# A graph network layer: the low-numbered sources of two aggregation steps by products with count matrices in place of row gathers

## The chip, the cores and the metric

The kernel runs on one core of a Trainium2 chip. The metric is the device time of one execution in microseconds (us), the median of three executions. A profile of one execution gives the busy times of the engines: PE (TensorE, products), DVE (VectorE), ACT (ScalarE), POOL (GpSimd) and the DMA queues that POOL, ACT and SP (SyncE) feed.

## What is computed

There are N = 10000 nodes with 512 float32 features, and E = 160000 directed edges, sorted by destination; a node has 16 incoming edges in the mean. The program is a relational graph layer with a feed-forward part, and after it two SAGE steps (the "last two steps"). The reference, cut to those two steps:

```python
def _sage_layer(h, src, dst, W_self, W_neigh, b, n_nodes):
    agg = segment_sum(h[src], dst, num_segments=n_nodes)       # sum the source rows of each node
    deg = segment_sum(ones_like(dst), dst, num_segments=n_nodes)
    h_neigh = agg / maximum(deg, 1.0)[:, None]
    return relu(h @ W_self + h_neigh @ W_neigh + b)

h = _sage_layer(feats, src, dst, W_self1, W_neigh1, b1, n_nodes)   # step 0
h = _sage_layer(h, src, dst, W_self2, W_neigh2, b2, n_nodes)       # step 1
```

Ahead of them, the first layer computes five products per node (`self_W` and four `rel_W`), and sums for every edge the row of its source and its edge type, `h_all[src, edge_type]`, by destination; then layer norms and a 512-1024-512 feed-forward part with a GELU follow.

## The kernel before

The nodes are cut into 78 blocks of 128 and one of 16. The kernel has four stages in time: the node products (in which the lists of edges are built as well, beside the products), the aggregation of the first layer with the feed-forward part, step 0, and step 1.

A block sums its edges in two ways. The first 11 edges of each of its 128 nodes are read by 11 indirect DMAs ("own" gathers: lane p of the gather is node p of the block), and DVE adds the 11 tiles to the sum. What a node has beyond 11 goes to 5 further gathers whose lanes are in any order, and to two "tails" that 4 and 16 blocks share; those tiles are added by products with one-hot matrices, on PE. Every gather moves 128 rows of 2 KB.

```python
T = 11 * E // (16 * N)          # 11 own edges a node
OT = 5                          # 5 gathers of other edges a block; 3 in the last, short block
SPANS = (4, 16)                 # a tail for 4 blocks, and one for 16

def gather(b, table):
    def rows(n, idx, name="rows", bufs=RING):                  # RING = 28 row tiles
        t = gat.tile([P, D], F32, name=name, bufs=bufs)
        nc.gpsimd.indirect_dma_start(out=t[:n], in_=table, ...)            # L660
        return t[:n]
    ...                                                        # tails, others, then own
def sums(b, others, hot):
    for t in order:                                            # 5 others and 2 tails
        nc.tensor.matmul(pa[:r], hot[:, t, :r], others[t], ...)            # L687
def add(b, pa, mine):
    for t in mine:                                             # 11 own tiles
        nc.vector.tensor_tensor(pa[:r], pa[:r], t[:r], op=OP.add)          # L699
```

The loop of the last two steps (`h_d` is the step's input, `wss` and `wns` its weights; `transposed` makes four transposes on PE, L167, and a copy on ACT, L168):

```python
for i, b in enumerate(blocks):
    hot = hots(blocks[i + 1])                                  # L676, DVE
    pa, mine = held
    add(b, pa, mine)                                           # L699, DVE
    nc.scalar.activation(m[:r], pa[:r], AF.Copy, scale=rdeg)   # L1021, ACT
    for k in range(KC):                                        # KC = 4
        nc.tensor.matmul(po[:r], hT[:, k, :r], wss[:, k, :])   # L1025
    if before:
        finish(*before)        # 4 products with wns (L991), bias, relu, store of block i-1
    turn(blocks[i + 1])        # transposes of the next block's own rows hb
    held = begin(blocks[i + 1], hot, h_d)                      # gathers and L687 of the next
    transposed(psT, mT[:, :, :r], m[:r], r)
    before = (b, po, mT)
```

The node products, beside which the lists are built a part at a time (`next(step)`), from windows of the sorted edges; each product is evicted by DVE:

```python
nc.vector.tensor_tensor(h, h, bself[:r], op=OP.add)                        # L614
nc.vector.tensor_tensor(xg[:r, c, :], xg[:r, c, :], ln2b[:r], op=OP.add)   # L615
for j, w in enumerate([wself] + wrel):                         # 5 weights
    for k in range(KC):
        nc.tensor.matmul(pm[:r], hT[:, k, :r], w[:, k, :], ...)            # L620
    ... nc.vector.tensor_tensor(...)                           # L623 and L626, the eviction
...
if b0 + c >= 2:
    next(step, None)           # a part of the lists, once a block
```

Of the kernel before, what the change touches and what calls it, by code (L numbers as in the profile page):

```python
# [8 lines left out]
F32 = mybir.dt.float32  # L9
# [12 lines left out]
def kernel(  # L22
# [32 lines left out]

    nc = tc.nc
# [18 lines left out]


    T = 11 * E // (16 * N)
    OT = 5
    OT_LAST = 3
# [3 lines left out]

    ROUNDS = 12
    PAD = P

    W = 36
    TAGS = 4 + 3 * NL
    FAR = 2 * SPAN * P
    WT = 2 * W + TAGS  # L90
    assert N % P and R * N <= 1 << 16 and 2 * T + WT <= 2 * P and OT * WT <= 512
    assert (4 + 3 * NL) * NB <= 1024 and 3 * NL * NB <= 512
    assert 4 * OT * P <= R * N and OT_LAST < OT and full % 2 == 0

    def own(b):

        return T if b < full else 0

# [13 lines left out]

    ident = const.tile([P, P], F32, name="ident")
# [9 lines left out]


    row = const.tile([P, full, T], I32, name="row")
    orow = const.tile([P, NB, OT], I32, name="orow")
    srow = [const.tile([P, -(-full // n)], I32, name=f"srow{i}") for i, n in enumerate(SPANS)]
    loc = const.tile([P, NB, OT + NL], F32, name="loc")
    fits = const.tile([1, 1], I32, name="fits")
    bad = const.tile([P, 5], F32, name="bad")  # L130
# [39 lines left out]
    def runs(ep, ep2, pse, found):  # L170
# [137 lines left out]
        nc.vector.tensor_tensor(deg, first[:, 1:], first[:, :P], op=OP.subtract)  # L308

# [25 lines left out]
        bounds = ep.tile([NB, 3 * NL, P], F32, name="bounds")  # L335
        nc.vector.tensor_copy(first_over, over)
        done = 0
        for lv, n in enumerate(SPANS):
# [22 lines left out]
            for i, v in enumerate((ov, upto)):  # L361
                w = bounds[:, 3 * lv + i, :]
                nc.vector.tensor_scalar(w, bounds[:, 3 * lv - 3 + i, :] if lv else v,
                                        float(-P if lv else -OT * P), 0.0, op0=OP.add, op1=OP.max)
                nc.vector.tensor_scalar(w, w, skip, None, op0=OP.add)
            nc.vector.tensor_scalar(bounds[:, 3 * lv + 2, :], ov, shift, 64.0, op0=OP.add,
                                    op1=OP.add)
            nc.vector.tensor_scalar(bounds[:, 3 * lv + 2, :], bounds[:, 3 * lv + 2, :], 0.0, None,
                                    op0=OP.max)
            yield  # L370
        for names, vs in ((("first", "deg", "from", "upto"), (first[:, :P], deg, ov, upto)),
                          ([f"{k}{lv}" for lv in range(NL) for k in ("sfrom", "supto", "sbase")],
                           [bounds[:, i, :] for i in range(3 * NL)])):
            pt = pse.tile([P, 512], F32, name="pe")
            for i, v in enumerate(vs):
                nc.tensor.transpose(pt[:, i * NB:(i + 1) * NB], v, ident[:NB, :NB])
            for i, name in enumerate(names):
                nc.vector.tensor_copy(found[name], pt[:, i * NB:(i + 1) * NB])

        nc.vector.memset(bad[:, 3:5], 0.0)  # L380
# [3 lines left out]
        nc.vector.tensor_scalar(bad[:NB, 3:4], upto_b, float(-P), over, op0=OP.is_lt, op1=OP.add)  # L384
        nc.vector.tensor_reduce(room, deg, op=OP.max, axis=mybir.AxisListType.X)
        nc.vector.tensor_tensor(room, room, lanes_b, op=OP.subtract)
        nc.vector.tensor_scalar(bad[:NB, 4:5], room, float(W), None, op0=OP.is_gt)
        pf = pse.tile([P, 512], F32, name="pe")
        nc.tensor.matmul(pf[:1, :5], ones[:, :1], bad, start=True, stop=True)
        count = ep.tile([1, 1], F32, name="count")  # L390
        nc.vector.tensor_reduce(count, pf[:1, :5], op=OP.add, axis=mybir.AxisListType.X)
        nc.vector.tensor_scalar(fits, count, 0.0, None, op0=OP.is_equal)
# [4 lines left out]
    def lists(ep, ep2, pse, found):  # L397

        tags = ep.tile([P, NB, TAGS], F32, name="tags")
        tag_i = ep.tile([P, NB, TAGS - 2], I32, name="tag_i")  # L400
        nc.vector.memset(tags[:, :, 0:1], 1.0)
        nc.gpsimd.iota(tags[:, :, 1], pattern=[[0, NB]], base=0, channel_multiplier=1,
                       allow_small_or_imprecise_dtypes=True)
        for i, n in enumerate(SPANS):
            of = tag_i[:, :, 2 + 2 * NL + i]
            nc.gpsimd.iota(of, pattern=[[1, NB]], base=0, channel_multiplier=0)
            nc.vector.tensor_scalar(of, of, n - 1, None, op0=OP.bitwise_and)
        for i, name in enumerate(["from"] + [f"sbase{lv}" for lv in range(NL)]):
            hi, lo = tag_i[:, :, 2 * i], tag_i[:, :, 2 * i + 1]
            nc.vector.tensor_copy(lo, found[name])  # L410
            nc.vector.tensor_scalar(hi, lo, 4, None, op0=OP.logical_shift_right)
            nc.vector.tensor_scalar(lo, lo, 15, None, op0=OP.bitwise_and)
        nc.vector.tensor_copy(tags[:, :, 2:], tag_i)
        nc.vector.memset(orow[:, full:, :], 0)
        nc.vector.tensor_scalar(rdeg, found["deg"], 1.0, None, op0=OP.max)
        nc.vector.reciprocal(rdeg, rdeg)
        iota_s = ep.tile([P, OT * P], F32, name="iota_s")
        nc.gpsimd.iota(iota_s, pattern=[[1, OT * P]], base=0, channel_multiplier=0,
                       allow_small_or_imprecise_dtypes=True)
        of_span = ep.tile([P, SPAN], F32, name="of_span")  # L420
        nc.gpsimd.iota(of_span, pattern=[[P, SPAN]], base=0, channel_multiplier=0,
                       allow_small_or_imprecise_dtypes=True)
        slot = ep.tile([P, OT], F32, name="slot")
        nc.gpsimd.iota(slot, pattern=[[P, OT]], base=0, channel_multiplier=1,
                       allow_small_or_imprecise_dtypes=True)
        nowhere = ep.tile([P, T], I32, name="nowhere")
        nc.gpsimd.iota(nowhere, pattern=[[0, T]], base=N * R, channel_multiplier=R)
        zero = ep.tile([P, D], F32, name="zero")
        nc.gpsimd.memset(zero, 0.0)
        for r in range(R):  # L430
            nc.sync.dma_start(hall_d[N:, r * D:(r + 1) * D], zero)
        nc.sync.dma_start(h1_d[N:, :], zero)
        nc.sync.dma_start(h2_d[N:, :], zero)

        kept, beyond = [], [None] * NL

        def between(low, high, b, n, out):

            after = ep2.tile([P, OT * P], BF16, name="after")
            if isinstance(out, str):  # L440
                out = ep2.tile([P, OT * P], BF16, name=out)[:, :n]
            nc.vector.tensor_scalar(after[:, :n], iota_s[:, :n], low[:, b:b + 1], None,
                                    op0=OP.is_ge)
            nc.vector.scalar_tensor_tensor(out, iota_s[:, :n], high[:, b:b + 1], after[:, :n],
# [3 lines left out]
        def picked(pm, at, base, place):  # L448


            n = at.shape[1]
# [26 lines left out]

        def read(b0):


            n = min(2, NB - b0)
            at = ep.tile([P, 2], I32, name="at", bufs=5)
# [13 lines left out]

        def look_up(b0, nb, win):
            halves = win.rearrange("p b j -> p (b j)").bitcast(BF16).rearrange(
                "p (b j) -> p b j", b=2)[:, :nb]  # L500
            ours, t0 = slice(b0, b0 + nb), own(b0)

            nc.vector.tensor_copy(halves[:, :, 2 * (t0 + W):2 * (t0 + W) + TAGS], tags[:, ours])

            if t0:
                few = ep2.tile([P, 2, T], I32, name="few")
                nc.vector.scalar_tensor_tensor(row[:, ours], halves[:, :, 0:2 * T:2], 256.0,
                                               halves[:, :, 1:2 * T:2], op0=OP.mult, op1=OP.add)
                nc.vector.tensor_tensor(few, found["deg"][:, ours].unsqueeze(2).to_broadcast(
                    [P, nb, T]), lane[:, None, :T].to_broadcast([P, nb, T]), op=OP.is_le)  # L510
                nc.vector.copy_predicated(row[:, ours], few,
                                          nowhere[:, None, :].to_broadcast([P, nb, T]))
            for c in range(nb):
                nt = OT if b0 + c < full else OT_LAST
                of = between(found["from"], found["upto"], b0 + c, nt * P, "of")
                pm = pse.tile([P, OT, WT], F32, name="pe")
                for t in range(nt):
                    nc.tensor.matmul(pm[:, t, :], of[:, t * P:(t + 1) * P],
                                     halves[:, c, 2 * t0:2 * t0 + WT], start=True, stop=True)
                got, rows, none = picked(pm[:, :nt], slot[:, :nt], 0, 2)  # L520
                nc.vector.tensor_tensor(loc[:, b0 + c, :nt], got[:, :, 1], none, op=OP.add)
                nc.vector.tensor_copy(orow[:, b0 + c, :nt], rows)
            if not t0:
                return

            for c in range(nb):
# [817 lines left out]
```

## Time and profile before

The three executions took 7276.59, 7280.13 and 7287.77 us; the median is 7280.13. The profiled execution has a span of 7287.9 us and a mean granted PE clock of 0.878 of full speed. The four stages, cut where the trace shows the first instructions of the next one:

| stage | from, to (us) | length | PE busy | DVE busy | POOL busy |
|---|---|---|---|---|---|
| node products, lists | 0 to 1590 | 1590 | 1483.7 | 915.6 | 84.3 |
| first aggregation, feed-forward | 1590 to 3575 | 1985 | 1704.3 | 1224.7 | 1250.8 |
| step 0 | 3575 to 5431 | 1856 | 1233.6 | 735.8 | 1228.8 |
| step 1 | 5431 to 7288 | 1857 | 1208.9 | 782.1 | 1242.6 |

How to read it: busy time is time in which an engine executed. For PE it is made of pipelined products whose ends are modelled, so the distance from the start of one product to the start of the next says more than the mean of one. For POOL, busy time holds the part of an indirect DMA that the engine itself works on, without the short gap that follows each of them; the moving of the rows is in the DMA columns.

### The profile page before, as it was taken

The page shows a single profiled execution, that of the slowest core. Times are in us where ns is not written, and L with a number is a line of the kernel's source. Part 1 is how long each engine was busy: PE and PEld are TensorE (multiplying, and loading weights), DVE is VectorE, ACT ScalarE, POOL GpSimd, SP SyncE. Part 2 cuts the span into 40 slices and gives each one's busy share as a digit, 9 for nine tenths or more (in the row PEclk, how much of TensorE's full clock was granted, in tenths as well). Part 3 has the DMA queues.
Part 4 walks back from the last instruction along what each step waited for, and adds up shares of the span by engine and source line. Part 5 has one row for each costly group of instructions (what it writes and reads, how often), then busy time and mean ns, then how long its engine had stood idle before and what let it go on. Part 6 is the DMA issues. An engine that isn't in the chain of part 4 may idle for free.

```text
span 7287.9 us, 49954 instructions
## 1 busy us (share of the span) xinstructions
PE 5630.5 (77%) x14251; PEld 2543.5 (35%) x14251; DVE 3658.1 (50%) x7302; ACT 1016.8 (14%) x1667; POOL 3806.5 (52%) x3927
## 2 busy tenths in 40 slices
PE   8999999976899888897676666666666666666666
PEld 3444444433334333343333233333232233332232
DVE  5457777334666666665344344333333444444444
ACT  1000000002233223232211011001010000000000
POOL 0000010026666666666266666666656666666665
PEclk9999999987999999998888888888887888887888
DMA  4222222246677777776366666666666777777775
GB/s 156 101 99 99 104 94 93 93 142 191 214 222 225 227 218 225 225 228 207 125 199 207 207 207 208 207 207 204 207 205 206 218 220 218 218 217 216 221 220 171
DMA packets 456993, 1361.47 MB, mean 187 GB/s; under 512 B 71746, under 2 KB 71746, under 8 KB 446578
## 3 DMA queue, kind: packets, MB, share of 16 engines
q0 software_dynamic: 308768, 1008.91, 46.8%
q1 hardware_dynamic: 136146, 266.29, 10.3%
q10 hardware_dynamic: 11792, 82.97, 2.8%
q8 instruction: 114, 1.87, 0.1%
q14 instruction: 173, 1.42, 0.1%
HBM read 1150.89 MB, written 207.01 MB: 186 GB/s over the span
## 4 chain that ended last, share of the span: by engine, by line
PE 34%; issue 21%; another core or an unknown queue 19%; ACT 3%; DVE 3%; POOL 2%; DMA 2%; ACTq 0%; POOLq 0%; DVEq 0%; SPq 0%
PE pa L687 9%; PE ph L783 6%; PE pm L620 5%; PE po L794 5%; PE po L991 3%; PE po L1025 3%; DVE pa L699 2%; POOL rows L660 2%; PE pT L167 1%; ACT hTb L168 1%; DMA rows<-h_d,row 1%; ACT mTb L168 1%; ACT mb L1021 0%; PE pT L771 0%
## 5 line engine op out<-in xcount | busy, mean ns | idle before, releaser
L699 DVE TENSOR_TENSOR pa<-pa,rows 128x512 f32<-128x512 f32 x2574 | 1798.6, 699 | 906.1 <-issue 571.5
L660 POOL DMA_INDIRECT rows<-h_d,row x1716 | 1669.4, 973 | 906.0 <-issue 423.0
L1025 PE MATMUL po<-wss,hTb 128*128 128x512 f32 (+1 forms) x1264 | 710.5, 715 | 652.1 <-ACT hTb L168 536.3
L687 PE MATMUL pa<-rows,hot 128*128 128x512 f32 (+1 forms) x2358 | 1096.2, 611 | 55.5 <-issue 31.9
L660 POOL DMA_INDIRECT rows<-hall_d,row x858 | 855.9, 998 | 492.6 <-issue 196.3
L620 PE MATMUL pm<-wrel,hT 128*128 128x512 f32 (+1 forms) x2528 | 1101.0, 593 | 14.4 <-DVE ha L623 14.4
L991 PE MATMUL po<-wns,mTb 128*128 128x512 f32 (+1 forms) x1264 | 662.0, 673 | 439.0 <-ACT mTb L168 306.3
L660 POOL DMA_INDIRECT rows<-h_d,orow x786 | 754.6, 960 | 400.8 <-issue 218.9
L620 PEld LDWEIGHTS pm<-wrel,hT 128*128 128x128 f32 (+1 forms) x2528 | 478.0, 189 | 622.1 <-issue 595.9
L687 PEld LDWEIGHTS pa<-rows,hot 128*128 128x128 f32 (+1 forms) x2358 | 458.9, 195 | 665.2 <-issue 631.6
L783 PE MATMUL ph<-x1T,w1s 128*128 128x512 f32 (+2 forms) x1344 | 587.0, 590 | 117.9 <-ACT hid L785 88.4
L1025 PEld LDWEIGHTS po<-wss,hTb 128*128 128x128 f32 (+1 forms) x1264 | 277.8, 231 | 1024.0 <-ACT hTb L168 589.5
L660 POOL DMA_INDIRECT rows<-hall_d,orow x393 | 373.3, 950 | 450.3 <-SPq L1340 326.5
L794 PE MATMUL po<-w2s,hid 128*128 128x512 f32 (+1 forms) x1264 | 560.9, 595 | 30.5 <-issue 23.2
L991 PEld LDWEIGHTS po<-wns,mTb 128*128 128x128 f32 (+1 forms) x1264 | 266.8, 216 | 816.2 <-issue 483.0
L687 PE MATMUL pa<-tail,hot 128*128 128x512 f32 x936 | 469.0, 617 | 78.0 <-issue 72.7
L997 DVE TENSOR_TENSOR po<-po,bss 128x512 f32<-128x512 f32 (+1 forms) x79 | 55.0, 696 | 805.5 <-remote 705.9
L493 POOL DMA_INDIRECT win<-rec_d,at x79 | 74.9, 948 | 719.7 <-issue 631.4
L623 DVE TENSOR_TENSOR ha<-pm,brel 128x512 f32<-128x512 f32 (+1 forms) x316 | 217.1, 687 | 424.1 <-PE pm L620 424.0
L783 PEld LDWEIGHTS ph<-x1T,w1s 128*128 128x128 f32 x1344 | 259.8, 201 | 414.1 <-issue 311.4
L1001 DVE TENSOR_TENSOR ob<-po,bss 128x512 f32<-128x512 f32 (+1 forms) x79 | 54.5, 689 | 663.4 <-remote 293.6
L794 PEld LDWEIGHTS po<-w2s,hid 128*128 128x128 f32 (+1 forms) x1264 | 236.2, 190 | 313.4 <-issue 301.8
(238 smaller groups left out, 4165.3 us busy)
## 6 DMA issues: line engine op xcount, KB each, us to landing
hall_d<-ha ACTq DMA_DIRECT2D x78, 1024.0 KB
hb<-h_d SPq DMA_DIRECT2D x38, 1024.0 KB
rows<-h_d,row POOLq DMA_INDIRECT x1716
xs<-xs_d SPq DMA_DIRECT2D x39, 512.0 KB
xr<-xr_d SPq DMA_DIRECT2D x39, 512.0 KB
xn_d<-xr SPq DMA_DIRECT2D x39, 512.0 KB
h_d<-h SPq DMA_DIRECT2D x39, 512.0 KB
xg<-in_x_dram SPq DMA_DIRECT2D x19, 1024.0 KB
```

The costliest lines, as they stand in the source:

```text
L167: nc.tensor.transpose(p[:, k, :r], rows[:, k * P:(k + 1) * P], ident[:r, :r])
L168: nc.scalar.copy(dest, p[:, :, :r])
L493: nc.gpsimd.indirect_dma_start(out=win[:, c, :], out_offset=None, in_=rec_d, in_offset=bass.IndirectOffsetOnAxis(ap=at[:, c:c + 1], axis=0))
L620: nc.tensor.matmul(pm[:r], hT[:, k, :r], w[:, k, :], start=(k == 0), stop=(k == KC - 1))
L623: nc.vector.tensor_tensor(ha[:r, j - 1, :], pm[:r], brel[:r, (j - 1) * D:j * D], op=OP.add)
L660: nc.gpsimd.indirect_dma_start(out=t[:n], out_offset=None, in_=table, in_offset=bass.IndirectOffsetOnAxis(ap=idx, axis=0))
L687: nc.tensor.matmul(pa[:r], hot[:, t, :r], others[t], start=(t == order[0]), stop=(t == order[-1]))
L699: nc.vector.tensor_tensor(pa[:r], pa[:r], t[:r], op=OP.add)
L783: nc.tensor.matmul(ph[:, :n], w1s[:, k, f * P:(f + 1) * P], self.xT[:, k, :n], start=(k == 0), stop=(k == KC - 1))
L794: nc.tensor.matmul(po[:r], self.hid[:, f, c * r:(c + 1) * r], w2s[:, f, :], start=(f == 0), stop=(f == FC - 1))
L991: nc.tensor.matmul(po[:r], mT[:, k, :r], wns[:, k, :], start=False, stop=(k == KC - 1))
L1025: nc.tensor.matmul(po[:r], hT[:, k, :r], wss[:, k, :], start=(k == 0), stop=False)
```

## The change

Of the edges in the last two steps, about a fifth come from the first 2048 nodes (16 blocks of 128 sources). Those edges are no longer gathered. For each destination block a matrix of counts, 2048 sources by 128 destinations, says how often a source feeds a destination; the sum of those edges is then 16 products of a 128x128 count tile with 128 resident rows of the input (`lows`, 4 MB on chip, loaded once a step). With a fifth of the edges gone, the lists of the rest are shorter: 9 own gathers and 4 others, with the tails 13.3 a block where there were 16.3.

- In the node products, six edges per node at most are scattered as ones (bfloat16, 2 bytes) into the count matrices in DRAM, which are zeroed first: six scatters a block from POOL. A node's low sources beyond the sixth, or repeated ones, stay in the lists. DVE finds the low sources and orders the rest (`part`), the rest is written to DRAM, and the lists for the last two steps are made from it in step 0 (`second_list`), beside its first and later blocks.
- The first layer keeps its lists. The first 16 blocks of step 0 and the short block use them too; the other 62 blocks of step 0 and the 78 of step 1 use counts.
- Two adds a block in the node products move from DVE to POOL; the lists are advanced six times a block (at first three times) instead of once; RING becomes 26; loads and stores of the last two steps are made for two blocks and not for four, to make room.

The diff, cut to its core:

```diff
-    T = 11 * E // (16 * N)
-    OT = 5
+    LB = 16
+    LOW = LB * P
+    CAP = 6
+    ls1 = Lists(11 * E // (16 * N), 5, 36)
+    ls2 = Lists(9 * E // (16 * N), 4, HIGHS - 9 * E // (16 * N))
...
+    count_d = [dram.tile([CELLS + 8 * P, 1], BF16, name=f"count_d{b}") for b in range(full)]
...
+        def part(b0, halves):
+            ...                       # keys of two blocks' windows, the 8 largest low ones (max),
+            for c in range(2):        # their cells
+                for j in range(CAP):
+                    st = nc.gpsimd.indirect_dma_start(
+                        out=count_d[b0 + c], in_=ones_b, in_offset=None,
+                        out_offset=bass.IndirectOffsetOnAxis(ap=at[:, c, j:j + 1], axis=0))
+            for c in range(2):        # the rest in order: 5 rounds of match_replace and max
+                for i in range(HIGHS // 8):
+                    nc.vector.match_replace(...)
+                    nc.vector.max(out=take, in_=now)
...
-                nc.vector.tensor_tensor(h, h, bself[:r], op=OP.add)
-                nc.vector.tensor_tensor(xg[:r, c, :], xg[:r, c, :], ln2b[:r], op=OP.add)
+                nc.gpsimd.tensor_tensor(xg[:r, c, :], xg[:r, c, :], ln2b[:r], op=OP.add)
...
+                        nc.gpsimd.tensor_tensor(h, h, bself[:r], op=OP.add)
+                    if b0 + c >= 2 and (paced or j in (1, 3)):
+                        next(step, None)
...
-        RING = 28
+        RING = 26
...
+            for k, (count, rows) in enumerate(counts):
+                nc.tensor.matmul(pa, count, rows, start=(k == 0), stop=False)
             for t in order:
-                nc.tensor.matmul(pa[:r], hot[:, t, :r], others[t], start=(t == order[0]),
-                                 stop=(t == order[-1]))
+                nc.tensor.matmul(pa[:r], hot[:, t, :r], others[t],
+                                 start=(t == order[0] and not counts), stop=(t == order[-1]))
...
+                def load_counts(b):
+                    if b < full and list_of(b) is ls2:
+                        raws[b] = ip.tile([P, LOW], BF16, name="raw")
+                        nc.sync.dma_start(raws[b], count_d[b][:CELLS, :]...)
+                def counts(b):
+                    for k in range(0, LB, LB // 2):
+                        t = ip.tile([P, LB // 2, P], F32, name="count")
+                        nc.scalar.copy(t..., raw[:, k * P:(k + LB // 2) * P])
+                        got += [(t[:, i, :], lows[:, k + i, :]) for i in range(LB // 2)]
+                lows = lp.tile([P, LB, D], F32, name="lows")
+                nc.sync.dma_start(lows, h_d[:LOW, :].rearrange("(k p) d -> p k d", p=P))
...
+                    next(making, None)                # step 0: a block of the second lists
                     if i + 1 < len(blocks):
                         turn(blocks[i + 1])
-                        held = begin(blocks[i + 1], hot, h_d)
+                        held = begin(list_of(blocks[i + 1]), blocks[i + 1], hot, h_d, counted)
```

## The prediction, made before the changed kernel ran

> **What bounds the kernel now.** The first view is the page's busy tenths in 40 slices of 182 us.
>
> ```profile
> PE   8999999976899888897676666666666666666666
> POOL 0000010026666666666266666666656666666665
> PEclk9999999987999999998888888888887888887888
> DMA  4222222246677777776366666666666777777775
> ```
>
> The first quarter (node products) belongs to PE. In the last half, where the change saves work, nothing reaches 9: PE, POOL and DMA all stand at 6 to 7. So the bound there must be read from single instructions. The busy times by stretch fix the stages (columns: stretch, length, busy us of PE, weight loads, DVE, ACT, POOL, clock, DMA share, GB/s).
>
> ```profile
> 0.00:1590.00 1590.00, 1483.72 (x4243) 685.82 (x4243) 915.59 (x3131) 111.59 (x182) 84.29 (x104) 0.97 0.28 103
> ...
> 3575.00:5431.00 1856.00, 1233.60 (x2994) 554.26 (x2994) 735.78 (x1036) 186.49 (x323) 1228.82 (x1276) 0.82 0.68 204
> 5431.00:7288.00 1857.00, 1208.87 (x2994) 546.36 (x2994) 782.06 (x1095) 139.09 (x238) 1242.55 (x1276) 0.82 0.70 215
> ```
>
> Then the groups by line and shape from 5700 to 7000 us, and POOL's timeline:
>
> ```profile
> L660 POOL DMA_INDIRECT rows<-h_d,row x616 | 605.8, 984 | 323.8 <-issue 152.3 <-remote 134.3 <-DMA rows<-h_d,orow 14.3
> L699 DVE TENSOR_TENSOR pa<-pa,rows 128x512 f32<-128x512 f32 x616 | 430.5, 699 | 148.2 <-issue 129.0
> L660 POOL DMA_INDIRECT rows<-h_d,orow x277 | 263.6, 952 | 84.4 <-issue 65.5 <-DMA rows<-h_d,row 10.1 <-DMA rows<-h_d,orow 4.9
> ...
> L687 PE MATMUL pa<-rows,hot 128*128 128x512 f32 x558 | 248.6, 592 | 0.0
> ...
> L687 PE MATMUL pa<-tail,hot 128*128 128x512 f32 x223 | 105.0, 593 | 0.0
> ```
> ```profile
> 5316.01 0.95 POOL L660 DMA_INDIRECT rows<-h_d,row  x1 [0.30 <-issue]
> 5317.26 0.95 POOL L660 DMA_INDIRECT rows<-h_d,row  x1 [0.30 <-issue]
> ```
>
> 616 own gathers at 11 a block are 56 blocks in 1300 us: **23.2 us a block**. With 277 others and 18 tails (a row not shown) POOL issues 16.27 gathers a block, each 1.254 us after the last (0.95 and a gap of 0.30): 20.4 us. So POOL is the bound of these steps, with 2.8 us a block lost in waits for a free row tile. PE's side comes from its timeline over one block:
>
> ```profile
> 3654.46 0.66 PE L167 MATMUL pT<-ident,hb 128*128 128x128 f32 x4
> 3654.95 1.88 PE L687 MATMUL pa<-tail,hot 128*128 128x512 f32 x4
> 3656.67 4.45 PE L687 MATMUL pa<-rows,hot 128*128 128x512 f32 x10
> 3660.96 0.60 PE L167 MATMUL pT<-ident,mb 128*128 128x128 f32 x4
> 3661.40 3.60 PE L1025 MATMUL po<-wss,hTb 128*128 128x512 f32 x8
> 3664.83 3.60 PE L991 MATMUL po<-wns,mTb 128*128 128x512 f32 x8
> 3668.27 0.60 PE L167 MATMUL pT<-ident,hb 128*128 128x128 f32 x4
> ...
> 3689.79 5.99 PE L991 MATMUL po<-wns,mTb 128*128 128x512 f32 x8 [11.04 <-ACT mTb L168]
> ```
>
> Two things carry the whole prediction. First, a block's 7 one-hot products are 14 instructions here, and the 4 products with wss are 8: **each float32 product is two PE instructions**. Second, from 3661.40 to 3664.83 eight take 3.43 us: 0.429 us each, **0.86 us a product**, at full clock. A block costs PE 3668.27 - 3654.46 = 13.8 us; 9.4 of the 23.2 us are free. The page's mean of 592 ns is not that distance, since products overlap.
>
> **What the Trainium skill says.** (1) "TensorE: Matmul & The Clock Gate", section Back-to-back issue gap, gives 518 cycles at 2.4 GHz for a warm 512-column product in bfloat16, some 216 ns. The trace's float32 instruction takes 429 ns, two such passes, and there are two of them, so a float32 product costs four. (2) The same page, Part 1: The HAM clock gate: after an idle window of some 3.4 us PE falls to half clock. The trace agrees: after 11.04 us idle the same eight instructions start in 5.9 us, not 3.4. A full PE has no such penalty. (3) "Perfetto Trace Analysis", What "DMA-bound" means: an issuing engine's track solid with DMA slices shows descriptor generation, not movement. The POOL lines agree. (4) "GPSIMD Engine Reference", section 4.1 Engine selection: POOL is about twice as slow as DVE in two-input elementwise work. No run here shows it yet; DVE's 0.69 us would make an estimate of 1.4 us for each moved add.
>
> **The change, part by part.**
>
> *POOL, last two steps.* 13.3 gathers x 1.254 = 16.7 us a block, 3.7 less. Over 62 + 78 = 140 blocks: 420 gathers, 527 us. That is what the change could bring if POOL stayed the bound.
>
> *DVE and ACT.* Two adds of 0.70 us a block go. ACT gets two copies of 128x1024 a block; its 128x512 copies take 0.59, so about 1.1 each, beside some 2.5 us of other work. Neither comes near the block time. In step 0 DVE also makes the second lists, about 6 us a block by the present list rows: 6 + 9 x 0.70 + about 2.5 = 15.
>
> *PE, last two steps.* Added: 16 products x 2 x 0.429 = 13.7 us; the count tile and `lows` are both float32, as in L687. Removed: one other gather's product, 0.86. So 13.8 + 13.7 - 0.9 = **26.7 us a block**. That is more than the old block (23.2), and than POOL's 16.7: PE becomes the bound, 3.5 us a block slower. The second lists add six bfloat16 products, about 0.07 each, 0.4 us in step 0. I see no wait that breaks the chain: by program order the next counts, `m` and hT are ready while PE does the 13 us of wss, wns and transposes or counts, and with 13 rows a block a ring of 26 holds two whole blocks. For small waits I take 0.3 us a block.
>
> *Bytes.* 13.3 x 0.262 MB + 0.52 for counts + 0.52 to 0.79 for loads and stores are some 4.6 MB a block, 170 to 180 GB/s at 26.7 us, under today's 204 to 215. Not a bound. `lows` (4 MB at some 200 GB/s) lies bare at the start of step 1 only: about 15 us.
>
> *Node products.* PE's 20 products a block (17.2 us) do not change. POOL gets six scatters: with the window, 7 x 1.25 + 2 x 1.4 = 11.6 us of about 19.5. DVE gets about 45 small instructions for two blocks; list instructions of that size take 0.15 to 0.34 us now, so at 0.2 about 4.5 us a block, less 2 x 0.69: +3.1. 915.6 + 78 x 3.1 = 1157 of 1590 us, 73%. So PE stays the bound, with somewhat more evictions that come late, while the finer steps remove some of the present 54 us (a row not shown) that PE waits there for the list's DVE work. Net +25 us, my least sure term. The lists' last part stands before the last four blocks in program order, so no long tail should be bare.
>
> *First aggregation.* Same gathers and products; a ring of 26 only cuts slack: +5.
>
> *Sum:* step 0: 62 x (26.7 + 0.4 + 0.3 - 23.2) = 260, and 10 for 16 old blocks on the smaller ring. Step 1: 78 x (26.7 + 0.3 - 23.2) = 296, and 15. With +25 and +5: 610. 7280 + 610 is about **7890 us**, 8% slower.
>
> **Rivals.** (a) *The gathers' gain arrives.* If a count product took one instruction, PE would need 13.8 + 6.9 - 0.9 = 19.8 us, level with POOL's 16.7 and its waits; some 3.2 us x 140 = 450 off, 6830 us. For it: POOL is plainly the bound, and PE has 9.4 us free. Against: the instruction counts above. (b) *The node products become bound by DVE or POOL.* If scatters cost 2 us or DVE's small instructions 0.35, those blocks go from 20 to 22 us or more: 150 us on top, 8040. For it: while lists are made, DVE already is some 75% busy. (c) *The PE chain breaks* on late counts or transposes; each wait over 3 us also costs clock. At 29 us a block: 8200. Against: the two-blocks-ahead loads. (d) *A warm clock helps more than thought.* My 13.8 is already at full clock, so nothing more is there; at best stage 1 gains 50 and the waits vanish: 7770.
>
> **Range and chances.** PE's floor, 140 x 3.5 = 490 us, rests on two measured numbers, so the low end is 7770; (b) and part of (c) set the high end, 8080. Faster by over 2% needs rival (a): 0.03. Within 2%: 0.02. Slower: 0.95.
>
> **What would show it.** Right: in the last two steps PE at 9 with clock near 1.0, and a block with 44 PE instructions of 512 columns for its sums (16 counts and 6 one-hots, two each) beside 16 for the weights; 26.7 to 27.5 us a block, POOL with long idle stretches that wait for PE, step 1 near 2170 us, step 0 near 2125. Wrong: 16 instead of 32 count instructions a block, PE waiting for ACT's count copies, or a first stage longer by over 100 us with PE waiting for DVE.

## The result, and the profile after

The changed kernel takes 8837.12 us (median of four runs, 8822.27 to 8859.35) against 7283.01 for the kernel before in the same comparison: a ratio of **1.214, 95% interval 1.211 to 1.217**. It is slower, as predicted, but by 1554 us and not by some 610. The prediction's range (7770 to 8080) doesn't hold it.

The profile after, in the prediction's order. First the busy tenths of the page, now in slices of 221 us:

```profile
PE   7446656656858989989966899999997999999999
POOL 1333333333256666666546444444443444544453
PEclk9777878778979999999978899999998999999999
DMA  3884445434356777777657555555555555555554
```

The right half is what was predicted: PE at 9 at a full clock, POOL down to 4. The left quarter is not. PE, at 9 there before, stands at 4 to 6 for some 2000 us, and *no other engine is near 9*; DMA reaches 8 in two slices and stays at 3 to 5 in the others. Such a stage waits for something that these rows don't show as busy. The stretches of the trace give the sizes (columns as before: stretch, length, busy us of PE, weight loads, DVE, ACT, POOL, clock, DMA share, GB/s):

```profile
0.00:2482.00 2482.00, 1559.02 (x4254) 714.25 (x4254) 1140.18 (x5059) 130.60 (x260) 760.04 (x770) 0.82 0.50 82
2482.00:4484.00 2002.00, 1704.24 (x4022) 753.22 (x4022) 1232.91 (x2063) 584.55 (x932) 1250.48 (x1276) 0.91 0.69 211
4484.00:6700.00 2216.00, 1970.59 (x5322) 904.50 (x5322) 1102.44 (x2998) 310.24 (x440) 1053.15 (x1098) 0.94 0.54 167
6700.00:8835.00 2135.00, 2093.61 (x5334) 953.82 (x5334) 667.40 (x937) 293.49 (x393) 1025.17 (x1041) 0.99 0.57 179
```

| stage | before | predicted | after |
|---|---|---|---|
| node products, lists | 1590 | 1615 | **2482** |
| first aggregation | 1985 | 1990 | 2002 |
| step 0 | 1856 | 2125 | 2216 |
| step 1 | 1857 | 2170 | 2135 |

867 of the 947 us by which the prediction was exceeded lie in the first row. There DMA moves *fewer* bytes a second than before (82 GB/s against 103) and yet its engines are busy for 0.50 of the time instead of 0.28: each byte holds an engine for longer. The costliest groups of the page carry the rest (line, engine, operation, operands, count, busy us, mean ns, idle us ahead of it and what ended that):

```profile
L886 PE MATMUL pa<-lows,count 128*128 128x512 f32 x4480 | 1970.4, 598 | 24.5 <-ACT count L1261 24.5
...
L859 POOL DMA_INDIRECT rows<-h_d,orow x646 | 612.4, 948 | 1677.2 <-PE pa L889 1464.5
...
L683 POOL DMA_INDIRECT count_d<-ones_b,cells x468 | 467.5, 999 | 587.9 <-DMA count_d<-ones_b,cells 245.6
```

4480 is 140 blocks x 16 products x 2: two PE instructions a count product, as predicted. POOL's gathers of the last two steps idle 1464.5 us until PE has used a row tile, so PE is the bound there. The last row is new: the scatters themselves wait for earlier scatters. In POOL's, PE's and DVE's timelines of the node products (start, length, engine, line, operation, then idle time before it and its releaser) it looks like this:

```profile
1539.53 0.20 POOL L678 COPY cells<-uncounted 128x16 int32<-128x16 int32 x1 [19.69 <-DMA count_d<-ones_b,cells]
...
1541.11 1.00 POOL L633 DMA_INDIRECT win<-rec_d,at  x1 [0.16 <-issue]
...
1545.02 0.26 DVE L644 SCALAR_TENSOR_TENSOR key<-win 128x96 f32<-128x96 bf16 x1 [23.83 <-DMA win<-rec_d,at]
...
1548.78 11.65 PE L816 MATMUL pm<-wrel,hT 128*128 128x512 f32 x22 [13.94 <-DVE ha L819]
```

A chain of three: POOL waits 19.69 us for a scatter to end; DVE waits 23.83 us for a window of edges that POOL reads; PE waits 13.94 us for DVE, whose next instruction in program order is the window's first use (L644), so that no product is evicted (L819) until the window is there. PE is named as waiting for DVE, but DVE is idle too. The question for the chip is what stands at the head of the chain.

### The profile page after: what moved, and what is told of

The parts are those of the page before. It is cut to its first block, busy times and chain, and to the rows that moved or that the text cites. A ratio compares the mean times of both kernels' runs of the same rounds, so it can differ in the third digit from the quotient of the medians.

```text
span 8834.9 us, 63717 instructions
## 1 busy us (share of the span) xinstructions
PE 7327.5 (83%) x18932; PEld 3325.8 (38%) x18932; DVE 4142.9 (47%) x11057; ACT 1318.9 (15%) x2025; POOL 4088.8 (46%) x4184
## 4 chain that ended last, share of the span: by engine, by line
PE 42%; issue 4%; DVE 2%; DMA 1%; another core or an unknown queue 1%; ACT 0%; SPq 0%; ACTq 0%; DVEq 0%
PE pa L886 21%; PE pa L889 8%; PE po L1230 5%; PE po L1296 5%; PE pT L198 1%; DVE pa L897 1%; DMA raw<-count_d 0%; DMA found<-found_d 0%; DVE ob L1240 0%; PE pT L573 0%; DVE both L503 0%; DVE after L474 0%; DVE hot L875 0%; PE pT L552 0%
## 5 line engine op out<-in xcount | busy, mean ns | idle before, releaser
L897 DVE TENSOR_TENSOR pa<-pa,rows 128x512 f32<-128x512 f32 x2294 | 1603.3, 699 | 2469.3 <-issue 2093.8
L886 PE MATMUL pa<-lows,count 128*128 128x512 f32 x4480 | 1970.4, 598 | 24.5 <-ACT count L1261 24.5
L859 POOL DMA_INDIRECT rows<-h_d,row x1436 | 1416.6, 986 | 510.0 <-issue 386.3
L859 POOL DMA_INDIRECT rows<-h_d,orow x646 | 612.4, 948 | 1677.2 <-PE pa L889 1464.5
L886 PEld LDWEIGHTS pa<-lows,count 128*128 128x128 f32 x4480 | 850.6, 192 | 1044.5 <-issue 1019.8
L889 PE MATMUL pa<-rows,hot 128*128 128x512 f32 (+1 forms) x2078 | 979.9, 616 | 75.7 <-DVE hot L875 31.7
L683 POOL DMA_INDIRECT count_d<-ones_b,cells x468 | 467.5, 999 | 587.9 <-DMA count_d<-ones_b,cells 245.6
L1296 PE MATMUL po<-wss,hTb 128*128 128x512 f32 (+1 forms) x1264 | 575.7, 598 | 13.3 <-ACT hTb L199 13.3
L816 PE MATMUL pm<-wself,hT 128*128 128x512 f32 (+1 forms) x632 | 332.9, 674 | 242.4 <-ACT hT L199 230.6
L199 ACT COPY mTb<-pT 128x512 f32<-128x512 f32 (+1 forms) x158 | 91.9, 582 | 2465.3 <-PE pT L198 2356.5
```

The costliest lines, as they stand in the source:

```text
L199: nc.scalar.copy(dest, p[:, :, :r])
L683: st = nc.gpsimd.indirect_dma_start(out=count_d[b0 + c], in_=ones_b, in_offset=None, out_offset=bass.IndirectOffsetOnAxis(ap=at[:, c, j:j ...
L816: nc.tensor.matmul(pm[:r], hT[:, k, :r], w[:, k, :], start=(k == 0), stop=(k == KC - 1))
L859: nc.gpsimd.indirect_dma_start(out=t[:n], out_offset=None, in_=table, in_offset=bass.IndirectOffsetOnAxis(ap=idx, axis=0))
L886: nc.tensor.matmul(pa, count, rows, start=(k == 0), stop=False)
L889: nc.tensor.matmul(pa[:r], hot[:, t, :r], others[t], start=(t == order[0] and not counts), stop=(t == order[-1]))
```

## Experiments

The length of the node products is read from the start of the first gather of the next stage, that of step 1 from the step's first loads. The runs fell in two sets in which transfers differ in speed whatever the kernel (the kernel before takes 7283 to 7335 us in one and 6619 to 6631 in the other; the same first aggregation moves 211 GB/s in one and 243 in the other), so times are compared within a set only: **S** marks the first, **F** the second. Where part of the work is left out, it is said.

### Which part of the change holds up the node products (set F)

Theory A: the scatters' list of cells has three buffers, and POOL waits for a buffer until scatters have read it. Edit:

```diff
-            at = ep.tile([P, 2, 8], I32, name="cells", bufs=3)
+            at = ep.tile([P, 2, 8], I32, name="cells", bufs=39)
```

> The changed kernel, except that the tile of scatter addresses has 39 buffers (one for each pair of blocks) instead of 3, so that the copy that refills it never waits for the scatters that read it. Theory A (in POOL's order that copy stands behind the pair's 12 scatters and waits 16 to 28 us for the last of them to land; window reads stand behind it, DVE behind the windows, PE behind DVE's evictions): the node products fall from 2482 us to 1650-1900 and the wait of the key operation for its window from some 690 us to under 250. Theory B (DVE has simply too much to do with the new small instructions, or POOL's adds slow it): stays at 2350-2500. Theory C (the 2-byte scatters clog the DMA engines, whoever waits): stays at 2200-2480, the waits only change place. Steps 0 and 1 unchanged in all, 2216 and 2135.

Theory B: the added work of DVE and POOL. Here no scatter is issued; the zeroing of the tables, DVE's work and the count products stay (low edges are left out of the sums):

```diff
-                for j in range(CAP):
+                for j in range(0):
```

> The changed kernel without the 468 scatters; the count matrices stay zero, so the edges of the low sources are left out of the sums; the number and the kind of all other instructions are as before. Theory A and theory C: node products at 1580-1680 us. Theory B: stays above 2300 us, since all of DVE's and POOL's other work is still there. The count products run on zeros, so steps 0 and 1 stay at 2216 and 2135 us within 2%.

Moving the two adds of a block from POOL back to DVE:

> The changed kernel with the two adds a block of the node products back on DVE. If the moved adds were the trouble (they wait in POOL's queue behind scatters, and the stores of their tiles and the next loads behind them: ACT shows 417 us of waits for the store of hg), the node products fall by 300 us or more from 2482. Theory A: POOL still blocks the windows, DVE gets 107 us more work, so 2400-2550. Steps unchanged.

And without the count products (low edges left out), for the last two steps:

> The changed kernel without the 16 count products a block; counts are still loaded and copied, so the sums lack the edges of the low sources. My sum for PE (13.8 + 13.7 - 0.9 = 26.7 us a block, PE the bound): without the products PE needs 12.9 us and POOL 16.7, and the block falls to 17-20 us, step 1 from 2135 to 1400-1600 us and step 0 from 2216 to 1550-1800. If instead something else holds the steps (the loads of counts, ACT's copies, the second lists), they stay above 1850. Node products unchanged at 2482.

Measured in us:

| run | node products | step 0 | step 1 | total |
|---|---|---|---|---|
| 39 buffers of cells | 2385 | 2116 | 2133 | 8396 |
| no scatters | **1601** | 2116 | 2132 | 7606 |
| adds back on DVE | 2427 | 2118 | 2135 | 8437 |
| no count products | **2484** | 1429 | **1350** | 7020 |

The run without count products leaves the node products as they are in the changed kernel, so its 2484 us are their length in set F with three buffers of cells (2482 in set S: the sets hardly differ in this stage). *A explains 99 us* (2484 - 2385): POOL's wait for cells, 547 us in all in the changed kernel, is gone with 39 buffers, but the stage is still 2385 us long. *B falls*: with all of DVE's and POOL's other added work the stage takes 1601 us, near the 1590 of the kernel before (read in set S; it has no profile in set F). So the scatters cost 883 us (2484 - 1601), and the adds on POOL 57 (2484 - 2427). The count products alone make the last steps longer: without them POOL's 13.3 gathers run at 17.1 us a block (1350 / 79), against the predicted 16.7. Both steps then lie under the expected spans, which had been drawn from set S. What is left is theory C of the first expectation: the scatters clog the transfers, whoever waits.

How do 468 scatters of 128 writes of 2 bytes (256 bytes a scatter) hold up a stage? The DMA view lists other transfers' median time from issue to landing (last column). With scatters (39 buffers, 800 to 2200 us):

```profile
q10 hardware_dynamic: 6480, 47.19, 33.3%
...
q0 software_dynamic: 12128, 3.71, 2.7%
...
hall_d<-ha ACTq DMA_DIRECT2D x45, 1024.0 KB, 21.2
xr_d<-xg SPq DMA_DIRECT2D x12, 1024.0 KB, 4.2
xs_d<-hg SPq DMA_DIRECT2D x11, 1024.0 KB, 19.0
...
high_d<-word SPq DMA_DIRECT2D x28, 40.0 KB, 17.3
```

Without scatters (500 to 1500 us):

```profile
q10 hardware_dynamic: 7488, 54.53, 13.2%
...
hall_d<-ha ACTq DMA_DIRECT2D x52, 1024.0 KB, 3.9
xs_d<-hg SPq DMA_DIRECT2D x13, 1024.0 KB, 4.2
xr_d<-xg SPq DMA_DIRECT2D x12, 1024.0 KB, 4.3
...
high_d<-word SPq DMA_DIRECT2D x28, 40.0 KB, 1.6
```

Stores that have nothing to do with the scatters, on other queues, land five to ten times later in the median; not all of them do, as `xr_d` shows. The queue rows (packets, MB, share of the 16 engines' time) say the same: q10 holds the `hall_d` stores alone, 158 us of engine time a MB with scatters and 39 without (33.3% of 16 x 1400 us over 47.19 MB, 13.2% of 16 x 1000 us over 54.53 MB), while the scatters' own queue, q0, takes only 2.7%. So the head of the chain is that transfers themselves slow down, in the DMA engines or in the memory behind them (the profile doesn't part the two), and not a buffer of the program.

### Which writes cost (sets S and F)

First the changed kernel itself, for reference in set S:

> The changed kernel unchanged, on the same chip as the runs beside it, so that they can be compared with it. No theory is told apart by it: node products should end some 880 us later than in the kernel before on the same chip, step 1 should take 2130 to 2140 us.

It gave 2482 us of node products and 8856 in total. Three runs then ask whether the cost goes by number or by size. Half of the scatters (`range(CAP // 2)`; the low edges of the other half are left out):

> Three scatters a block instead of six, the first three of each node's sources (the other low edges are left out). If the cost goes by the number of small writes, and the DMA engines have no room to hide them: 880 / 2 = 440 us fewer, node products end near 2040. If some of the writes hide in idle DMA time and only the excess shows: under 1900. If any scatter at all puts the chain of window reads behind (a fixed wait per block): over 2250.

Rows of 512 bytes instead of single elements, in tables of their own (low edges left out; `slots` is lane + 128 j, which keeps the rows of one table apart). The size comes from the Trainium skill, "DMA: Bandwidth & Descriptors", section Specifications, by which a write under 512 bytes is a read, a change and a write:

```diff
+            nc.vector.scalar_tensor_tensor(at, at, 15 << 10,
+                                           slots[:, None, :].to_broadcast([P, 2, 8]),
+                                           op0=OP.bitwise_and, op1=OP.bitwise_or)
-                        out=count_d[b0 + c], in_=ones_b, ...      # rows of 1 bfloat16
+                        out=wide_d[(b0 + c) % 16], in_=ones_b, ...  # rows of 256 bfloat16
```

> As many scatters with as many writes to as scattered places, but each write is a row of 512 bytes instead of 2, to tables of their own (the counts stay zero, so low edges are left out). Theory that it is the smallness of a write that costs[...]: node products fall to 1600 to 1800 us, 30 MB more to move notwithstanding. Rival theory, that the cost is the number of writes at whatever size: node products stay at about 2400 to 2500 us.

Its control, the same indices and tables with rows of one element:

> The control of the run with rows of 512 bytes: the same indices, the same separate tables, but rows of 2 bytes again (counts stay zero, low edges left out). If the size of the write is what made the difference (2482 to 1804 us), node products end again at 2300 to 2500. If it was the separate tables or their indices, they stay near 1800.

Rows of 64 bytes:

> The same again with rows of 64 bytes. Theory that every write under 512 bytes is a read, a change and a write, whatever its size: node products end at 2300 to 2500 us, as with 2 bytes. Rival theory, the cost is in writes that share a short stretch of memory with others (64 bytes or less): they end at 1750 to 1900, as with 512 bytes.

And 2-byte writes that all go to the spare cells, side by side (low edges left out):

> Six scatters a block with 2-byte writes as in the changed kernel, but every write goes to the spare cells: the 128 writes of a scatter lie side by side in 256 bytes (counts stay zero, low edges are left out). If scattered places cost (a new stretch of memory for each write): node products end at 1600 to 1800 us. If the cost goes by the writes' number and smallness, wherever they go: 2300 to 2500. If writes to one short stretch wait for each other: later than 2500.

| run (set S) | node products, us |
|---|---|
| six scatters, 2 bytes (the changed kernel) | 2482 |
| three scatters, 2 bytes | 1747 |
| six, rows of 512 bytes | 1804 |
| six, rows of 64 bytes | 1805 |
| six, rows of 2 bytes, same indices | 2526 |
| six, 2 bytes, side by side | 2901 |

512 bytes a write cost no more than 64, although they move 30 MB instead of 4, and 680 to 720 us less than 2 bytes. So the theory drawn from the skill (2300 to 2500 for 64 bytes) falls: these runs show no step between 64 and 512 bytes. Two results spoke for another reading. Half of the scatters cost far less than half (1747, not 2040), and writes side by side cost most of all. So the suspicion moved from small writes to small writes that *crowd* into one place. Two runs in set F put it to the test. Each 2-byte write with 64 bytes of memory to itself (the control's indices times 32; low edges left out):

> As the control with rows of 2 bytes (node products 2526 us), but each index times 32, so that every write of 2 bytes has a stretch of 64 bytes of memory for itself (counts stay zero, low edges are left out). If it is the write of a part of a stretch that costs, whoever else writes there: 2400 to 2550 us, as the control. If it is several writes that meet in one stretch of 64 bytes: 1780 to 1850, as with rows of 64 bytes.

Rows of 32 bytes (low edges left out):

> As the run with rows of 64 bytes (1805 us), with rows of 32 bytes: where the size begins to cost. If a write must fill 64 bytes of memory to be cheap: 2300 to 2550 us. If 32 bytes are enough: 1780 to 1850.

No scatters, a second time, as their base line:

> The changed kernel without its scatters (low edges left out) once more, beside these runs: the first time it ran on a chip on which transfers are faster. It sizes what the six scatters cost when their writes are large (1805 us) in issues alone: node products should end at 1600 to 1650 us, so some 170 us for 468 issues of 1.25 us on GpSimd and the DVE work that they hold up. If it ends near 1800, large writes cost nothing, and the rest of the time is DVE's and GpSimd's added work.

Node products took **1749** us with lone 2-byte writes, **1736** with rows of 32 bytes, 1600 without scatters. The control (2526) was run in set S alone, but the changed kernel itself is as long in both (2482 and 2484). Two bytes are cheap when nothing else is written beside them.

That leads back to a detail of the change that the prediction had passed over. A list has room for six low edges a node; a place that holds none is sent to a spare cell, and these lay side by side:

```python
uncounted = ep.tile([P, 8], I32, name="uncounted")
nc.gpsimd.iota(uncounted, pattern=[[P, 8]], base=CELLS, channel_multiplier=1)
```

Counted in the input, 359 of a block's 768 writes go there, 128 x 2 bytes next to each other in each scatter; of the first three scatters' 384 only 72 do, since those places nearly always hold an edge. That fits the low cost of half of the scatters. The real cells, by contrast, lie all over 512 KB. Merely to share 64 bytes is not what costs: counted in the input, some 24,500 of the control's 31,900 writes for real cells share 64 bytes with another write of their scatter, against 500 in the changed kernel, and the control took only 44 us longer (2526 against 2482). How closely writes must crowd was not tested. One number moves the spare cells 64 bytes apart, with nothing left out:

```diff
-    count_d = [dram.tile([CELLS + 8 * P, 1], BF16, ...)
+    count_d = [dram.tile([CELLS + 32 * 8 * P, 1], BF16, ...)
-        nc.gpsimd.iota(uncounted, pattern=[[P, 8]], base=CELLS, channel_multiplier=1)
+        nc.gpsimd.iota(uncounted, pattern=[[32 * P, 8]], base=CELLS, channel_multiplier=32)
```

> The changed kernel with one number changed: the spare cells, to which a scatter sends the places of a list that hold no low edge, lie 64 bytes apart instead of side by side. By the input 359 of a block's 768 writes go to spare cells (72 of the first three scatters' 384, which fits that run's 150 of 880 us). Nothing is left out. If it is writes that meet in one short stretch that cost: node products end at 1750 to 1850 us instead of 2482 (on the chip state where the kernel before takes about 7300), total 8130 to 8230. If the real cells' scattered writes are the cost: node products stay at 2300 to 2500.

Node products: **1712 us**, 772 less than the 2484 of set F with spare cells side by side and the same three buffers of cells. Total 7712.25 us, 1.163 of the kernel before (1.161 to 1.165) in the same comparison. Its stretches (the first is cut 28 us into the gathers):

```profile
0.00:1740.00 1740.00, 1504.01 (x4282) 693.83 (x4282) 1150.82 (x5078) 132.32 (x262) 783.00 (x791) 0.94 0.33 123
1740.00:3504.00 1764.00, 1623.38 (x3998) 727.47 (x3998) 1220.37 (x2060) 581.82 (x931) 1265.44 (x1290) 0.96 0.76 243
...
5620.00:7710.00 2090.00, 2081.85 (x5312) 950.76 (x5310) 666.28 (x936) 290.87 (x390) 994.98 (x1011) 1.00 0.55 175
```

In its first row, the work of every engine is that of the changed kernel (DVE 1150.82 against 1140.18, POOL 783.00 against 760.04); PE's clock is back from 0.82 to 0.94. The chain of three is gone, as the waits show (us in total, times, longest). With spare cells side by side (39 buffers of cells, 400 to 2200 us):

```profile
DVE key L644 <- DMA win<-rec_d,at: 616.8, 34, 79.4
```

With spare cells 64 bytes apart (400 to 1600 us), where `hall_d` lands in 3.9 us again:

```profile
DVE key L644 <- DMA win<-rec_d,at: 96.8, 32, 8.6
```
```profile
hall_d<-ha ACTq DMA_DIRECT2D x34, 1024.0 KB, 3.9
```

Of the scatters' 883 us in set F, 772 are thus the spare cells' place, the wait for buffers of cells included, and 111 (1712 - 1601) are left for six scatters whose spare writes lie apart. In POOL's timeline they still follow each other at 1.27 us.

### The count products, and whether the change can pay

The counts are bfloat16 in memory, and ACT widened them to float32 for the product with float32 rows. Here the counts go in as they are, and the rows are split once a step into two bfloat16 halves, so that 32 products of one instruction replace 16 of two (two halves keep fewer bits than the float32 value they stand for). This run and those after it that use halves also have 39 buffers of cells:

```diff
-                        nc.scalar.copy(t, raw[...])               # counts to float32
-                        got += [(t[:, i, :], lows[:, k + i, :]) ...]
+                    return [(raw[:, k * P:(k + 1) * P], half[:, k, :])
+                            for k in range(LB) for half in (high, low)]
```

> The count products take the 16-bit counts as they are and the low rows as two 16-bit halves, 32 products of one instruction a block instead of 16 of two; ScalarE's copies of the counts fall away; the cells tile also has 39 buffers (which the earlier run showed to change little). Theory that TensorE's count products bound the steps at 2 x 0.429 us each: a 16-bit product of 512 columns should be 0.216 us, so the term of 13.7 us a block falls to 6.9, the step to about 20 us a block, 1580 to 1680 us for step 1 and 1650 to 1750 for step 0. Rival, the steps are held by the arrival of counts or by the gathers' contention with them: step 1 stays over 1900 us. Node products unchanged, about 880 us more than before.

Step 1 took 1625 us, inside the expected span; step 0, at 1842, was slower than expected (1650 to 1750). The total fell by 994 us to 7861 (set S), of which 107 are the buffers' (node products 2375 us instead of 2482). PE's timeline over a block of step 1:

```profile
7403.12 0.75 PE L198 MATMUL pT<-ident,mb 128*128 128x128 f32 x4
...
7411.23 0.38 PE L886 MATMUL pa<-lowlo,raw 128*128 128x512 bf16 x1
7411.45 0.38 PE L886 MATMUL pa<-lowhi,raw 128*128 128x512 bf16 x1
...
7417.92 1.88 PE L889 MATMUL pa<-tail,hot 128*128 128x512 f32 x4
...
7423.07 0.60 PE L198 MATMUL pT<-ident,mb 128*128 128x128 f32 x4
```

From 7411.23 to 7417.92, 31 products take 6.69 us, 0.216 us each, just the figure of the Trainium skill, "TensorE: Matmul & The Clock Gate", section Back-to-back issue gap, that the prediction named; the block takes 19.95 us. Rival (a) of the prediction had 19.8 for this case.

Both findings together were then run as candidates. Before the spare cells were understood, with three scatters and a longer list of the rest (set S):

> Two findings put together, as a version that might beat both kernels: three scatters a block (the low edges beyond a node's first three go to the list of the rest, which takes 10 own rows instead of 9, so 14.3 gathers a block), and the count products with 16-bit halves (32 one-pass products a block). From the runs with each alone: node products end near 1750 us, first aggregation 2010, step 0 1840 to 1900 (list of the rest still made beside it), step 1 1625 to 1680, as 14.3 x 1.254 = 17.9 us of gathers stay under the 20 us of products. Sum 7230 to 7360 us, against about 7300 for the kernel before: within 2% of it. If the gathers' own spacing bounds (23.2 us for 16.27 gathers in the kernel before, so 20.4 us for 14.3), 7250 to 7400.

It took 7440.24 us, a ratio of 1.012 (1.007 to 1.018): above the expected sum. Node products took 1697 us, but step 1 1716 instead of 1625 to 1680; why its 14.3 gathers cost more than their issue was not tested. With spare cells apart (set F), six scatters and then five:

> Spare cells 64 bytes apart and the count products with 16-bit halves of the low rows: both causes of the loss taken away, nothing left out. From the runs with each alone: node products 1780, first aggregation 2010, step 0 1840, step 1 1625, sum 7255 us against about 7300 for the kernel before, ratio 0.985 to 1.005 (where transfers are faster and the kernel before takes 6620: node products 1740, aggregation 1640, steps 1780 and 1610, sum 6770, ratio 1.02).

> As the run with spare cells apart and halves, with five scatters a block instead of six; the low edges beyond a node's fifth (0.12 a node by the input) go to the list of the rest, at the same 13.3 gathers a block. 78 scatters fewer at 1.25 us of GpSimd each, of which a part is on the path: node products 15 to 40 us shorter than with six, the rest equal. If the scatters that are left cost nothing, no difference.

| run (set F) | node products | step 1 | total | ratio to before (95%) |
|---|---|---|---|---|
| spare cells apart | 1712 | 2133 | 7712.25 | 1.163 (1.161 to 1.165) |
| and halves | 1686 | 1618 | 6735.25 | 1.016 (1.014 to 1.018) |
| and five scatters | 1646 | 1617 | 6696.52 | 1.010 (1.008 to 1.012) |

Both came out near what was expected (a ratio of 1.02, and 15 to 40 us less with five scatters). With both causes taken away, 1.27 (39 buffers of cells alone, 8396 / 6619) becomes 1.01. The rest of the loss has about the size of what the scatters still add (1646 - 1600 = 46 us, against 66 in total). The shorter gathers bring little here: taking 1590 us for its node products, as in set S, and 1750 for its aggregation, as in the run with spare cells apart, the kernel before has by estimate some 1645 us left for each of the last steps, 20.8 us a block, near the 20.4 of POOL's issues alone, and the halves put PE at 20. No version ran faster than the kernel before. The last two were not run in set S, where slower transfers make the gathers they save dearer; how they stand there is open.

## Why the prediction was wrong, point by point

- **The failed step: "Net +25 us", the node products.** Measured +892. The step counted the scatters only by what POOL pays to issue them (1.25 us each) and asked nothing of where their writes land. What the runs showed in its place: some 28,000 writes (359 x 78) of 2 bytes side by side slow down transfers of other queues and cost 772 of the 883 us, about 28 ns each (772 us / 28,000, an estimate from the two runs). The window reads arrive late, and DVE's order passes the wait on to PE. The other 111 us the step took to be hidden behind PE.
- The rest of that step was right. DVE was put at 1157 us and shows 1140.18; leaving out the scatters gives 1601, +11. The moved adds, estimated at 1.4 us, take 1.25 to 1.28, and moving them back saved 57 us while transfers were slow.
- *Rival (b)* named the right stage and the wrong limit: neither DVE (0.46 of the stage) nor POOL (0.31) is its bound. "A first stage longer by over 100 us with PE waiting for DVE" was named as a sign; it came, but DVE was waiting itself.
- *Step 1*: right. 2135 us against 2170, 27.0 us a block (2135 / 79) against 26.7 to 27.5, PE busy 0.98 at a clock of 0.99. Through all fourteen kernels and repeats that kept the float32 count products it stayed at 2130 to 2136 us in both sets: bounded by PE, it did not feel the speed of transfers. The ground for it, two instructions of 0.429 us a product, was borne out by taking the products away (1350) and by halving them (1625).
- *Step 0*: the mechanism was right, the size off by 91 us (2216 against 2125). Its first 16 blocks and the short one, still with gathers, took 449 us (4484 to 4933) where the same blocks before took 419 (3575 to 3994), 30 more and not 10. The other 62 take 28.5 us each (1767 / 62), not 27.4: PE is idle for 67 of the 1767 us, 1.1 a block where the prediction allowed 0.3, and the trace has 59 of them ahead of the second lists' products (L573), mostly until DVE has made their operands. So there the prediction's "I see no wait that breaks the chain" missed a small one. In set F, with the spare cells apart, the first blocks are 89 us shorter (357 against 446 from the load of `lows` to the first count product) and the other 62 at 28.4 each, so only the first blocks follow the transfers.
- *First aggregation*: 2002 against 1990, right.
- *The bound before*: the prediction put 2.8 us a block down to waits for a free row tile. Its lines name only "remote" for them, an unknown releaser, so that reading was not shown; by the estimate of 20.8 us a block in set F they all but vanish where transfers are faster.
- *Rival (a)*, the gathers' gain arrives, came true only with halves, on PE's block time (19.95 against 19.8).

## What to carry to other kernels

Where a scatter has nothing to write, don't park its writes side by side: spare elements 64 bytes apart cost some more memory and took 772 us away here. When a stage slows and no engine is busy, compare the time from issue to landing of transfers that have nothing to do with the change; if several rise, look at where the new writes land before adding buffers: 36 more saved 99 of the 883 us. And before a product is added to an engine with free time, count its instructions by the types of its operands: small counts need no float32, and a float32 operand split in two bfloat16 halves took half the PE time.

## What was not expected of the hardware

- Adjacent 2-byte writes cost the stage about 28 ns each (an estimate), and the 31,900 more of the run with all of them side by side 13 each (2901 - 2482 us), while a scatter that wrote 64 or 512 bytes a row, or 2 bytes 64 bytes apart, left the node products at 1712 to 1805 us. 32 bytes a row, side by side, are cheap too (1736). Sizes between 2 and 32 bytes were not tried, nor was it shown what the memory path does with writes that crowd.
- They slow others: an unrelated store of 1 MB landed in 21.2 us instead of 3.9.
- A float32 product of 512 columns takes 2 x 0.429 us, the same in bfloat16 0.216; two halves for a float32 operand are half the time.
